# A decoder on one core: seven block products for the cross attention's queries and for three quarters of the shared expert

## The chip, the cores and the metric

The kernel runs on one core of one Trainium2 chip. The metric is the time of one execution on the device in microseconds (us); a version is judged by the median of several runs. All arithmetic is float32.

## The reference, cut to what matters

Two decoder layers work on x of 8 batches x 256 tokens x 256 features. Layer 0 is self attention, a cross attention and an expert layer; layer 1 starts with a causal self attention. None of these is touched. What follows in layer 1 is (a function per batch b, P = 128):

```python
xn = layernorm(x[b])                      # 256 x 256
k, v = split(ctx[b] @ Wkv)                # ctx 256 x 512, Wkv 512 x 2048
q = xn @ Wq                               # Wq 256 x 1024, 16 heads of 64
o = softmax([q . null_key, q . k^T] / 8) @ [null_value; v]
x[b] += layernorm(o @ Wout, 1e-6) * ln_scale + ln_bias
# then, over all 2048 tokens
xe = layernorm(x)
gates, expert = top1(sigmoid(xe @ router))
routed = swiglu(xe * gates; w1, w3, w2 of that token's expert)
shared = (silu(xe @ ws1) * (xe @ ws3)) @ ws2          # ws1, ws3 256 x 704
out = x + routed + shared
```

## The kernel before

**Stages.** Layer 0 and layer 1's self attention run as units up to about 624 us. Then `null_cross_attention` (from line 1057) goes over the eight batches, then `token_experts` (from line 1423) finishes: rows are sorted by expert through HBM, 17 tiles go through their experts (`slots`), and x gets what comes back.

**A batch in the loop (from L1359).** `weighted` makes the scores (`stx`, L1228), their exponentials (ScalarE, L1232), the sums `den` (L1242) and the weighted values `ox` (L1266). Then the norm of the next batch is transposed (`layernorm_T`, tile `xn`), and the normed rows of the batch before for the experts (`routed_norm` and `routed_rows`, tile `xne`); both tiles share one tag with two buffers. Then come the next batch's keys and values. These two products are not done plainly: `seven` cuts left and right matrix into 2 x 2 blocks and makes seven block products in place of eight, with sums of blocks on both sides (`sums_of_context`, `sums_of_weights` on VectorE, DVE for short) and additions of the results when they leave PSUM. `k7` and `v7` are generators that issue these products in steps; a product that goes on in a bank must wait until ScalarE or DVE has read what stood there. The queries are plain: `queries` (L1205) makes the null key's scores `nps` and 64 half matmuls `fm`, whose results DVE copies to `qTx` (L1069). `divide` multiplies the attention by the reciprocals that come back through HBM (`rs`). `outward` (L1321) projects it (`wo`), ScalarE copies the result (`yx`, L1329), DVE takes its statistics, GpSimd (POOL) raises the variance to -1/2 (`lxrs`, L256), DVE norms, POOL multiplies by `lns` and adds `lnb` (L1334, L1335) and adds to x (L1336).

**Order.** Between `manual_schedule` and `order.close()` the order of TensorE (PE) is that of the code. Elsewhere, and for the other engines inside the loop, a planner picks among what it takes to be ready, earlier lines first, and the result is fixed in each engine's queue. On the chip a queue never overtakes: an instruction that waits holds up those behind it. Buffers of one tag are given out in the order of the code.

**Shared expert.** Its 2048 tokens are done in four quarters of 512 (`hidden_shared`, L947): 5 full chunks of 128 hidden features take 4 matmuls of 128x512 each, the last 64 features of both weights 2; ScalarE applies silu (L944), DVE multiplies (L945) into `mid`. Quarter 0 covers the last batch's division, quarter 1 its norm and the routing; there the tiles are called `hx`. Quarters 2 and 3 (`h`) stand in `token_experts`, quarter 3 as the last thing before the final output matmuls (L1442, L1453) and stores. In the last stage an expert's weights lie in tiles `w13` and `w2`, four buffers each.

In the profile a float32 matmul counts as two instructions, and `product` (L272) issues each matmul as two halves of 64 output rows that run side by side, so one product of a 128x128 block is four.

Of the kernel before, what the change touches and what calls it, by code (L numbers as in the profile page):

```python
# [38 lines left out]
P = 128  # L39
# [116 lines left out]
def plain(  # L156
# [105 lines left out]
    def layernorm_T(b, work, mm):  # L262

        xn = work.tile([P, 2, D], F32, tag="xn", name="xn")
        mv, rs = norm_stats([x[:, 2 * b + t, :] for t in range(2)], 1e-5, small, "ln")
        for t in range(2):
            last = normed(xn[:, t, :], x[:, 2 * b + t, :], mv, rs, t)
        return last, transposed(xn, work, mm, "xnT")
# [9 lines left out]
    def transposed(rows, work, mm, tag, dst=None):  # L278

        ps = mm.tile([P, 2, 2 * P], F32, tag="mm", name="tr")  # L280
        for t in range(2):
            for c in range(2):
                nc.tensor.transpose(ps[:, c, t * P : (t + 1) * P], rows[:, t, c * P : (c + 1) * P], ident)  # L283
        if dst is None:
            dst = work.tile([P, 2, 2 * P], F32, tag=tag, name=tag)
        nc.scalar.copy(dst, ps)  # L286
        return dst
# [472 lines left out]
    def weights_x():  # L760
# [4 lines left out]
        ctxs = wproj.enter_context(tc.tile_pool(name="ctxs", bufs=2, side="right"))  # L765
# [191 lines left out]

    def routed_norm(b, work):

        xn = work.tile([P, 2, D], F32, tag="xn", name="xne")  # L960
        mv, rs = norm_stats([x[:, 2 * b + t, :] for t in range(2)], 1e-5, small, "ln")
        for kept, v in zip(norms[b], (mv, rs)):
            nc.gpsimd.tensor_copy(kept, v)
        for t in range(2):
            normed(xn[:, t, :], x[:, 2 * b + t, :], mv, rs, t)
        return xn
# [90 lines left out]
    def null_cross_attention(phase):  # L1057
# [4 lines left out]
        def feature(dst, w, rows, copy, c2):  # L1062

            n = w.shape[1]
            ps = mm.tile([P, 2, S], F32, tag="mm", name="fm")
            for i in range(2):
                for cc in range(n):
                    product(ps[:, i, :], w[:, cc, (c2 + i) * P : (c2 + i + 1) * P], rows[:, cc, :], cc == 0, cc == n - 1)
            copy(dst[:, c2 : c2 + 2, :], ps)  # L1069

        def features(dst, w, rows, copy):
            for c2 in range(0, nc8, 2):
                feature(dst, w, rows, copy, c2)
# [6 lines left out]
        def keys(ctxT):  # L1080
            kT = work.tile([P, nc8, S], F32, tag="kT", name="kTx", bufs=1)
            features(kT, wkv_x, ctxT, nc.scalar.copy)
            return kT

        half = CTX // P // 2

        def w_block(j, k):

            return wkv_x.rearrange("p c (m k f) -> p c m k f", m=2, k=2)[:, half * j : half * (j + 1), :, k, :]

        tw = wsum.tile([P, 3, half, 2, XH * XD // 2], F32, name="tw")
        t1, t2, t3, t4 = tw[:, 0], tw[:, 1], w_block(0, 1), tw[:, 2]

        def sums_of_weights(n):
            dst, p, q = (
                (t1, w_block(0, 1), w_block(0, 0)),
                (t2, w_block(1, 1), t1),
                (t4, w_block(1, 0), t2),
                (t3, w_block(1, 1), w_block(0, 1)),
            )[n]  # L1100
            for m in range(2):
                for c in range(half):
                    nc.vector.tensor_tensor(dst[:, c, m], p[:, c, m], q[:, c, m], ALU.subtract)

        def sums_of_context(ctxT):


            def block(i, j):
                return ctxT[:, half * j : half * (j + 1), bass.ts(i, P)]

            sw = wsum.tile([P, 3, half, P], F32, tag="sw", name="sw")
            s1, s2, s3, s4 = sw[:, 0], sw[:, 1], block(1, 0), sw[:, 2]
            nc.vector.tensor_tensor(s1, block(1, 0), block(1, 1), ALU.add)
            nc.vector.tensor_tensor(s2, s1, block(0, 0), ALU.subtract)
            nc.vector.tensor_tensor(s4, block(0, 1), s2, ALU.subtract)
            nc.vector.tensor_tensor(s3, block(0, 0), block(1, 0), ALU.subtract)
            return block(0, 0), block(0, 1), s4, block(1, 1), s1, s2, s3

        w_terms = w_block(0, 0), w_block(1, 0), w_block(1, 1), t4, t1, t2, t3

        def seven(terms, m, dst):

            xy = scp.tile([P, 2, 2 * S], F32, tag="sc", name=f"kv{m}")
# [8 lines left out]
            def product_of(n, bank, fresh):  # L1132

                s, t = terms[n - 1], w_terms[n - 1][:, :, m, :]
                for i in range(4 if m == 0 else 1):
                    for c in range(half):
                        if m == 0:
                            args = bank[:, bass.ts(i, P)], t[:, c, bass.ts(i, P)], s[:, c, :]
                        else:
                            args = bank, s[:, c, :], t[:, c, :]  # L1140
                        for made in product(*args, fresh and i == 0 and c == 0, c == half - 1):
                            for other in (xb, yb):
                                for ins in read[id(other)] if other is not bank else ():
                                    tc.declare_no_dep(made.ins, ins.ins, reason="another bank")

            if m == 0:
# [7 lines left out]
            else:  # L1154

                def of(i, j):
                    return dst[:, i, 8 * j : 8 * j + 8, :]

                def seen(bank):
                    return bank.rearrange("p (h d) -> p h d", h=8)  # L1160

            def kept(bank, name):
                t = work.tile([P, 2 * S], F32, tag="pT", name=f"kv{name}{m}", bufs=4)
# [6 lines left out]
            zb = mm.tile([P, 2 * S], F32, tag="mm", name=f"kvz{m}")  # L1170
# [12 lines left out]
            reads(yb, nc.vector.tensor_tensor(of(0, 1), u, seen(yb), ALU.add))  # L1183
            product_of(4, xb, False)
# [3 lines left out]
        def vals(ctxT):  # L1188
            v = work.tile([P, 2, XH, XD], F32, tag="vx", name="vx", bufs=1)
# [13 lines left out]
            return v  # L1203

        def queries(xnT):  # L1205

# [5 lines left out]
            yield  # L1212
            qT = work.tile([P, nc8, S], F32, tag="qT", name="qTx", bufs=1)
            for c2 in range(0, nc8, 2):
                feature(qT, wq_x, xnT, nc.vector.tensor_copy, c2)
                if c2 == 0:
                    yield
            yield qT, en
# [102 lines left out]
        def outward(b, oT, en):  # L1321
# [9 lines left out]
            for t in range(2):  # L1331
                xt = x[:, 2 * b + t, :]
                normed(y[:, t, :], y[:, t, :], mv, rs, t)
                nc.gpsimd.tensor_tensor(y[:, t, :], y[:, t, :], lns, ALU.mult)  # L1334
                nc.gpsimd.tensor_tensor(y[:, t, :], y[:, t, :], lnb, ALU.add)  # L1335
# [6 lines left out]
        def silu(n):  # L1342
            return work.tile([P, 2 * S], F32, tag="pT", name="slx", bufs=4)[:, :n]

        def quarter(q):
            return hidden_shared(q, pair, silu)


        _, xnT = layernorm_T(0, work, mm)
        ctxT = context(0)  # L1350
        kT = keys(ctxT)
        for n in range(3):
            sums_of_weights(n)
        v = vals(ctxT)
        *_, (qT, en) = queries(xnT)
        sums_of_weights(3)
        load_router()
        order = ExitStack()
        for b in range(B):  # L1359
# [4 lines left out]
            if more:  # L1364
                _, xnT = layernorm_T(b + 1, work, mm)
                terms = sums_of_context(ctxT)
            else:
                rest()
# [4 lines left out]
                routing_tables(late)  # L1373
                order.enter_context(tc.manual_schedule(engines={mybir.EngineType.PE}))
            if b:
                routed_rows(b - 1, routed_norm(b - 1, work), work)
            if more:
                order.enter_context(tc.manual_schedule(engines={mybir.EngineType.PE}))
                kT = work.tile([P, nc8, S], F32, tag="kT", name="kTx", bufs=1)
                v = work.tile([P, 2, XH, XD], F32, tag="vx", name="vx", bufs=1)  # L1380
                k7, v7, q = seven(terms, 0, kT), seven(terms, 1, v), queries(xnT)
# [7 lines left out]
            if more:  # L1389

                for made in (k7, k7, v7, k7, k7, v7, v7):
                    next(made)
                if b:
                    routed_scores(b - 1)
                next(q)
                next(v7)
                next(v7)
            else:
                for i, _ in enumerate(quarter(0)):
# [4 lines left out]
            if more:  # L1404
                *_, (qT, en) = q
            order.close()
        with tc.manual_schedule(engines={mybir.EngineType.PE, mybir.EngineType.DVE}):
            for i, _ in enumerate(quarter(1)):
                if i == 1:
                    xn = routed_norm(B - 1, work)  # L1410
                if i == 2:
                    routed_rows(B - 1, xn, work)
                if i == 3:
# [9 lines left out]
    def token_experts(phase):  # L1423
# [21 lines left out]

        def quarter(q):
            for last in hidden_shared(q, pair, silu):
# [1189 lines left out]
```

## Time and profile before

| what | value |
| --- | --- |
| runs | 1377.36, 1377.01, 1377.0, 1373.41, 1374.71 us; median 1377.0 |
| profiled execution | 1376.14 us; its span, first to last instruction, 1374.4 us |
| granted clock, mean | 0.995 |
| busy, of the span | PE 97%, weight loads 66%, DVE 39%, ScalarE 33%, POOL 29% |
| one batch of the loop | 60.4 us (from 780.34 to 840.73 us and on), of which PE idles 0.32 us |
| queries of one batch, `fm` | 64 instructions of 128x256, 57.0 us in all for eight batches |
| quarters of the shared expert | `hx` 88 instructions of 128x512, 38.9 us; `h` 88, 38.2 us |

A row of the timeline has the start, the busy time, the engine, the line, the operation, the tile written <- tiles read, the shapes, the count, and in brackets the idle time of the engine before it and what ended that. A row of PE ends about 0.2 us after the next may begin, so the cost of a group is taken from its start to the start of the next.

### The profile page before, as it was taken

To read this page: it belongs to the slowest core of one execution; us is meant where nothing else is said; L and a number is where in the kernel's file an instruction comes from. 1 tells how busy PE (TensorE), PEld (TensorE's weight loads), DVE (VectorE), ACT (ScalarE), POOL (GpSimd) and SP (SyncE) were. 2 spreads that over 40 slices of the span, in tenths; PEclk is the share of its full clock that TensorE was granted. 3 is DMA by queue.
4 is the path that set the end of the run, shared out by engine and by line. 5 is a ranking of instruction groups with operands and counts; after the bars stand their busy time and mean duration, and the time that the engine had idled before them with its cause. 6 is when DMAs were issued, how large, how long until landed. Compare 5 with 4: busy or idle time off the path is not lost.

```text
span 1374.4 us, 30022 instructions
## 1 busy us (share of the span) xinstructions
PE 1334.7 (97%) x12814; PEld 901.9 (66%) x12814; DVE 533.9 (39%) x1539; ACT 456.8 (33%) x730; POOL 405.0 (29%) x513
## 2 busy tenths in 40 slices
PE   6999999999999999999999999999999999999998
PEld 3666756756766766764757566676756655788884
DVE  5443563473465555344223322232332236322223
ACT  2455443543553443431313222131322212022221
POOL 4322052051033243320324424152343512400004
PEclk9999999999999999999999999999999999999999
DMA  9970000000000004200011010101101110689954
GB/s 304 339 232 16 9 25 1 17 24 1 2 9 2 2 9 141 83 2 1 21 44 33 16 32 16 48 2 47 33 1 32 64 32 26 273 331 403 392 199 129
DMA packets 46926, 116.65 MB, mean 85 GB/s; under 512 B 8272, under 2 KB 30400, under 8 KB 42432
## 3 DMA queue, kind: packets, MB, share of 16 engines
q1 hardware_dynamic: 38912, 92.74, 19.9%
q0 software_dynamic: 5152, 18.89, 3.7%
q10 hardware_dynamic: 2720, 3.02, 0.6%
q8 instruction: 103, 1.69, 0.5%
q14 instruction: 39, 0.32, 0.1%
HBM read 104.00 MB, written 27.93 MB: 96 GB/s over the span
## 4 chain that ended last, share of the span: by engine, by line
PE 85%; DVE 5%; POOL 4%; issue 2%; ACT 1%; DMA 0%; ACTq 0%; POOLq 0%; DVEq 0%; SPq 0%
PE kv L274 11%; PE st L334 9%; PE o L366 9%; PE h L274 6%; PE fm L274 5%; PE wo L274 5%; PE ox L1266 4%; PE stx L1228 4%; PE out L1625 3%; PE out L1442 3%; PE h L952 3%; PE tr L283 3%; PE qk L274 3%; PE hx L952 3%; PE den L1242 2%; PE ao L274 2%
## 5 line engine op out<-in xcount | busy, mean ns | idle before, releaser
L366 PE MATMUL o<-pT,padv 128*64 128x256 f32 (+1 forms) x1536 | 172.1, 366 | 1.2 <-POOL pT L346 1.2
L343 ACT ACTIVATE pT<-st 128x1024 f32<-128x1024 f32 (+1 forms) x128 | 110.4, 915 | 88.2 <-PE st L334 87.4
L366 PEld LDWEIGHTS o<-pT,padv 128*64 128x64 f32 x1536 | 103.3, 137 | 53.9 <-issue 11.2
L334 PE MATMUL st<-qm,kT 64*128 64x256 f32 (+1 forms) x1024 | 116.3, 365 | 0.9 <-DVE qm L312 0.6
L334 PEld LDWEIGHTS st<-qm,kT 64*128 64x128 f32 x1024 | 89.2, 188 | 25.9 <-issue 15.6
L1234 POOL TENSOR_TENSOR both<-pTx 128x512 f32<-128x512 f32 x64 | 79.7, 1280 | 55.5 <-ACT pTx L1232 38.9
L1232 ACT ACTIVATE pTx<-stx 128x1024 f32<-128x1024 f32 x64 | 62.0, 1021 | 88.2 <-PE stx L1228 87.6
L274 PE MATMUL h<-xrT,w 128*64 128x128 f32 (+1 forms) x1936 | 87.0, 250 | 1.2 <-issue 1.2
L274 PEld LDWEIGHTS h<-xrT,w 128*64 128x64 f32 x1936 | 84.4, 137 | 4.0 <-issue 1.8
L256 POOL TENSOR_TENSOR lnrs<-lnve,mhalf 128x2 f32<-128x2 f32 x48 | 33.6, 701 | 150.9 <-DVE lnve L254 99.1
L343 ACT ACTIVATE pT<-st,kbias 128x1024 f32<-128x1024 f32 x64 | 68.0, 1112 | 28.8 <-PE st L334 28.7
L334 PE MATMUL st<-qm,memk 64*128 64x256 f32 x512 | 68.8, 393 | 0.5
L945 DVE TENSOR_TENSOR midr<-sl,h 128x128 f32<-128x128 f32 x102 | 29.3, 288 | 101.8 <-PE h L274 69.0
L944 ACT ACTIVATE sl<-h 128x128 f32<-128x128 f32 (+1 forms) x114 | 35.3, 310 | 96.0 <-PE h L274 56.5
L1228 PE MATMUL stx<-qTx,kTx 64*128 64x256 f32 x512 | 64.3, 391 | 2.5 <-ACT pTx L1232 2.5
L346 POOL TENSOR_SCALAR_AFFINE_SELECT pT<-pT 128x512 f32<-128x512 f32 x64 | 39.5, 638 | 83.0 <-ACT pT L343 79.8
L274 PE MATMUL qk<-l_wqkv,xnT 128*64 128x512 f32 x256 | 62.8, 612 | 0.7 <-ACT xnT L286 0.7
L1266 PE MATMUL ox<-pTx,vx 128*64 128x256 f32 x512 | 61.1, 381 | 0.0
L1228 PEld LDWEIGHTS stx<-qTx,kTx 64*128 64x128 f32 x512 | 46.1, 186 | 20.3 <-issue 9.2
L274 PE MATMUL wo<-wout_x,oT 128*64 128x256 f32 x512 | 58.0, 379 | 0.0
L334 PEld LDWEIGHTS st<-qm,memk 64*128 64x128 f32 x512 | 48.0, 186 | 15.1 <-issue 5.1
L1317 POOL TENSOR_TENSOR oT<-oT,rs 128x512 f32<-128x512 f32 x30 | 37.7, 1286 | 65.7 <-DMA rs<-rd 65.7
(312 smaller groups left out, 2222.1 us busy)
## 6 DMA issues: line engine op xcount, KB each, us to landing
w<-packs SPq DMA_DIRECT2D x22, 1408.0 KB
w<-packs SPq DMA_DIRECT2D x22, 768.0 KB
rs<-rd SPq DMA_DIRECT2D x16, 512.0 KB
packs<-L_ffn_w_eDF SPq DMA_DIRECT2D x8, 704.0 KB
packs<-L_ffn_w_eDF SPq DMA_DIRECT2D x8, 640.0 KB
packs<-L_ffn_w_eFD SPq DMA_DIRECT2D x8, 640.0 KB
ctxT<-ctx_T SPq DMA_DIRECT2D x8, 512.0 KB
wkv_x<-L_xattn_Wkv POOLq DMA_DIRECT2D x1, 4096.0 KB, 18.8
```

The costliest lines, as they stand in the source:

```text
L274: nc.tensor.matmul(out[h], lhsT[:, h], rhs, start=start, stop=stop, skip_group_check=True)
L283: nc.tensor.transpose(ps[:, c, t * P : (t + 1) * P], rows[:, t, c * P : (c + 1) * P], ident)
L334: nc.tensor.matmul(st[:, g, i, :n], kT[rows, c, bass.ts(kt, P)], qm[rows, 2 * mq + i, c, q0:], start=True, stop=True,)
L343: nc.scalar.activation(pT[:, :, :, :n], st[:, :, :, :n], AF.Exp, scale=scale, **kb)
L366: nc.tensor.matmul(o[64 * i : 64 * i + 64, mq, q0:], v_pad[:, kt, 4 * c + 2 * mq + i, 2 * g : 2 * g + 2, :], pTs[kt][:, g, i, : S - q0], s ...
L952: nc.tensor.matmul(h, shared["ws13"][:, c, lo : lo + P], shared["xnT"][:, c, bass.ts(q, 2 * S)], start=c == 0, stop=c == 1)
L1228: nc.tensor.matmul(st[:, g, kt, :], kT[rows, c, bass.ts(kt, P)], qT[rows, c, :], start=True, stop=True)
L1232: nc.scalar.activation(pT, st, AF.Exp, scale=scale)
L1234: nc.gpsimd.tensor_tensor(both, pT[:, :, 0, :], pT[:, :, 1, :], ALU.add)
L1266: nc.tensor.matmul(o[XD * g : XD * (g + 1), i, :], v[:, kt, 2 * (c2 + i) + g, :], pT[:, g, kt, :], start=kt == 0, stop=kt == 1, skip_group ...
L1442: nc.tensor.matmul(ps, mid[:, i, lo : lo + P], w2[:, i, :], start=i == 0, stop=i == NFC - 1)
L1625: nc.tensor.matmul(ps[h], mid[:, i, h], sets[k % len(sets)][1][:, i, :], start=i == 0, stop=i == NFC - 1, skip_group_check=True,)
```

## The change

1. **Queries.** `seven` gets a name, the terms of both sides and a flag for the layout, and makes the queries as well (`q7`): seven products of 4 x 1 blocks with 128 columns each in place of the 64 instructions of `fm`. Sums of Wq are made once (tile `twq`), sums of the normed rows for each batch on DVE (`swq`, four of 128x128). ScalarE now takes four of the results out of PSUM and DVE three, where DVE copied four. The first batch's queries stay plain.
2. **Order in the loop.** `q7`'s steps are woven between those of `k7` and `v7`; products 7, 3 and 4 come after `outward`, with the routing scores ahead of 4 and the null key's scores behind it. `routed_norm` is issued directly after `layernorm_T`, and `routed_rows` comes into PE's written order.
3. **Buffers.** `ctxT`, `xnT` and the tag `xn` (norm of the next batch and rows for the experts) have one buffer in place of two.
4. **Output norm.** The multiplication by `lns` and the addition of `lnb` go from POOL to DVE.
5. **Shared expert, quarters 0, 1 and 3.** `hidden_seven` makes the 5 full chunks of both weights in seven products, two chunks at a time (a, b, then c with one), 35 matmuls of 128x256 in place of 20 of 128x512; the last 64 features stay as they were. DVE makes four sums of the weights (128x640) before quarters 0 and 3 (quarter 1 uses the first ones) and four of the rows (128x256) for each quarter.
6. **End of the loop.** In the last batch `divide` and `outward` come after 15 of the 21 products of quarter 0; in quarter 1 the norm, the transposes and the scores of the last batch come one step earlier.

The core of the diff:

```diff
-    def layernorm_T(b, work, mm):
-        xn = work.tile([P, 2, D], F32, tag="xn", name="xn")
+    def layernorm_T(b, work, mm, bufs=2):
+        xn = work.tile([P, 2, D], F32, tag="xn", name="xn", bufs=bufs)
...
-        ctxs = wproj.enter_context(tc.tile_pool(name="ctxs", bufs=2, side="right"))
+        ctxs = wproj.enter_context(tc.tile_pool(name="ctxs", bufs=1, side="right"))
...
+    def hidden_seven(q, of_w, sx, mm, pair, spare):
...
+        def chunks(first, n):
+            xb, yb = pair(n * S)
+            (p1, p5), (u, sl) = ([t[:, k, : n * S] for k in range(2)] for t in (spare(), spare()))
...
+            product_of(1, xb, True)
+            read[id(xb)].append(nc.scalar.copy(p1, xb))
+            yield
+            zb = mm.tile([P, 2 * S], F32, tag="mm", name="hz")[:, : n * S]
+            product_of(2, zb, True)
+            nc.vector.tensor_tensor(p1, p1, zb, ALU.add)
+            nc.scalar.activation(p1, p1, AF.Silu)
+            yield
+            product_of(5, yb, True)
+            read[id(yb)].append(nc.scalar.copy(p5, yb))
+            yield
+            product_of(6, xb, False)
+            read[id(xb)].append(nc.scalar.copy(u, xb))
+            yield
+            product_of(7, xb, False)
+            read[id(xb)].append(nc.vector.tensor_tensor(p5, p5, xb, ALU.add))
+            yield
+            product_of(3, yb, False)
+            read[id(yb)].append(nc.vector.tensor_tensor(u, u, yb, ALU.add))
+            to_mid(0, u, p1)
+            yield
+            product_of(4, xb, False)
+            nc.scalar.activation(sl, xb, AF.Silu)
+            yield to_mid(1, sl, p5)
...
+        a, b = chunks(0, 2), chunks(2, 2)
+        for g in (a, a, a, a):
+            next(g)
+        yield
+        for g in (b, a, b, a):
+            next(g)
+        yield
+        for g in (b, a, b):
+            next(g)
+        c = chunks(4, 1)
+        yield
+        for g in (c, b, c, b):
+            next(g)
+        yield
+        for g in (c, b, c):
+            next(g)
+        ht = mm.tile([P, 2 * S], F32, tag="mm", name="ht")
+        end(0)
+        yield
+        next(c), next(c)
+        end(1)
+        last = next(c)
...
     def routed_norm(b, work):
-        xn = work.tile([P, 2, D], F32, tag="xn", name="xne")
+        xn = work.tile([P, 2, D], F32, tag="xn", name="xne", bufs=1)
...
-                nc.gpsimd.tensor_tensor(y[:, t, :], y[:, t, :], lns, ALU.mult)
-                nc.gpsimd.tensor_tensor(y[:, t, :], y[:, t, :], lnb, ALU.add)
+                nc.vector.tensor_tensor(y[:, t, :], y[:, t, :], lns, ALU.mult)
+                nc.vector.tensor_tensor(y[:, t, :], y[:, t, :], lnb, ALU.add)
...
             if more:
-                _, xnT = layernorm_T(b + 1, work, mm)
-                terms = sums_of_context(ctxT)
+                _, xnT = layernorm_T(b + 1, work, mm, 1)
+                if b:
+                    xe = routed_norm(b - 1, work)
+                of_ctx = sums_of_rows(ctxT, CTX // P // 2, "sw", False)
...
             if b:
-                routed_rows(b - 1, routed_norm(b - 1, work), work)
+                routed_rows(b - 1, xe, work)
             if more:
-                order.enter_context(tc.manual_schedule(engines={mybir.EngineType.PE}))
...
+                of_x = sums_of_rows(xnT, 1, "swq", True)
...
+                q7 = seven("q7", of_x, w_terms(q_blocks, 0), qT, False)
                 next(k7)
                 rest()
...
-                for made in (k7, k7, v7, k7, k7, v7, v7):
+                for made in (k7, k7, v7, k7, k7, k7, v7, v7, q7, v7, q7, v7, v7, q7):
                     next(made)
-                if b:
-                    routed_scores(b - 1)
-                next(q)
-                next(v7)
-                next(v7)
             else:
-                for i, _ in enumerate(quarter(0)):
+                shared["of_w"] = sums_of_shared(*(sums.tile([P, full * P], F32, name=f"tws{i}") for i in range(4)))
+                first = quarter(0)
+                for i in range(4):
+                    next(first)
                     if i == 0:
                         routed_scores(b - 1)
             divide(oT, rs, (nc.gpsimd, nc.gpsimd if more else nc.vector))
             outward(b, oT, old)
             if more:
-                *_, (qT, en) = q
+                next(q7), next(q7)
+                if b:
+                    routed_scores(b - 1)
+                next(q7)
+                en = null_key(xnT)
+            else:
+                for _ in first:
+                    pass
             order.close()
...
+        def beside():
+            return wts.tile([P, 2, FIRST], F32, tag="w13", name="beside")[:, :, : 2 * S]
...
+            sets = [wts.tile([P, NFC * D], F32, tag="w2", name=f"sums{i}") for i in range(3)]
```

A step of `seven` issues, call by call, the products 1 | 2 and 5 | 6 | 7 | 3 | 4; its evictions are ScalarE copies after 1, 5, 6 and 4 and DVE additions after 2, 7 and 3.

## The prediction

> **What bounds the kernel.** I read the page's busy shares first, then PE's timeline over one batch of the loop, then DVE's queue at the place where the change puts new evictions.
>
> ```profile
> PE 1334.7 (97%) x12814; PEld 901.9 (66%) x12814; DVE 533.9 (39%) x1539; ACT 456.8 (33%) x730; POOL 405.0 (29%) x513
> ...
> L274 PE MATMUL fm<-xnT,wq_x 128*64 128x256 f32 x512 | 57.0, 379 | 0.0
> L952 PE MATMUL hx<-xnTe,ws 128*128 128x512 f32 x88 | 38.9, 596 | 0.0
> ...
> 833.73 7.08 PE L274 MATMUL fm<-xnT,wq_x 128*64 128x256 f32 x64
> 840.73 2.00 PE L1228 MATMUL stx<-qTx,kTx 64*128 64x256 f32 x16
> ...
> 858.83 0.66 PE L283 MATMUL tr<-ident,xn 128*128 128x128 f32 x4
> 859.33 0.60 PE L283 MATMUL tr<-ident,xne 128*128 128x128 f32 x4
> 859.86 1.97 PE L274 MATMUL kv<-ctxT,wkv_x 128*64 128x128 f32 x32
> ...
> 869.47 1.92 PE L274 MATMUL kv<-ctxT,wkv_x 128*64 128x128 f32 x32
> 871.22 1.92 PE L274 MATMUL kv<-sw,wkv_x 128*64 128x128 f32 x32
> ```
>
> PE is full and no row here has idle time in brackets, so a matmul taken out is time taken out, and a wait put in is time put in. The clock was 0.995, so it plays no part. DVE and ScalarE have room in sum; what counts is the moment at which an eviction gets its turn.
>
> **Gains.** Queries: `fm` costs 840.73 - 833.73 = 7.00 us a batch, 64 instructions of 256 columns at 109 ns. The keys' products already have the shape of `q7`: from 869.47 to 871.22, 32 instructions of 128 columns, 54.7 ns each, half of 109, so a short matmul pays no extra. `q7` has 7 x 16 = 112 of them: 6.13 us, 0.87 less, for seven batches **6.1 us**.
>
> The Trainium skill ("TensorE: Matmul & The Clock Gate", Back-to-back issue gap) speaks against that: in a stream of weight loads and matmuls it gives some 81 ns a matmul at 128 columns and 131 at 512, so halving the columns doesn't halve the cost; by it 112 x 81 = 9.1 us would stand against the 7.0 of `fm`, a loss of some 15 us in seven batches. The trace has 54.7 ns for this very shape, side by side in halves, and decides.
>
> Shared expert: quarter 0 takes 434.7 ns for an instruction of 128x512 (36 of them from 1105.84 to 1121.49), so its 44 cost 19.13 us. The same full array at 256 columns stands in the output matmuls: the 84 from 1181.33 to 1199.46 take 216 ns each. A quarter then has 70 x 216 + 4 x 434.7 = 16.9 us, 2.2 less, for three quarters **6.5 us**. Further, the transposes of the last batch's rows waited 0.49 us at 1140.47. Now `outward` comes earlier with 4.8 us of products behind it and 3.5 of quarter 1, and the chain to the rows loses POOL's slower steps, so that wait goes: **0.5 us**. Together 13.1.
>
> **First cost, the shared buffer of xn and xne.** Rows for the experts can be normed only when the transposes of `xn` have read the one buffer, and PE's order has the transposes of `xne` next. The DVE copy of `ox` before it ends at 859.64, one norm instruction takes 0.41, the handover 0.08 (as at 8.03 to 8.12): PE goes on at 860.13 where it went on at 859.33, and the second half waits a little more, 0.84 us. Behind it in PE's queue stands everything of the next products. It falls on batches 1 to 6: **5.0 us**. Nothing: only if the transposes of `xn` were drawn ahead of the last `ox`, and PSUM tiles of their tag are given out in order. I keep 0 and 6 as ends.
>
> **Second cost, the eviction after q7's seventh product.** Product 4 goes on in the bank of product 7 and must wait for DVE's addition. Between stand product 3 (0.87 us) and, from batch 1 on, the scores (0.43); the addition takes 0.69 and 0.3 for both handovers. Were DVE free, nothing would wait. But `outward` has just ended, and DVE has its norm:
>
> ```profile
> 834.56 0.75 DVE L251 BATCH_NORM_STATS2 lxst<-yx 128x6 f32<-128x256 f32 x2 [7.95 <-ACT yx L1329]
> 835.23 0.30 DVE L252 BATCH_NORM_AGGREGATE lxmv<-lxst 128x2 f32<-128x6 f32 x2
> 835.56 0.17 DVE L254 TENSOR_SCALAR lxve<-lxmv 128x2 f32<-128x2 f32 x1
> 836.55 0.74 DVE L260 TENSOR_SCALAR yx<-yx,lxmv,lxrs 128x256 f32<-128x256 f32 x2 [0.81 <-POOL lxrs L256]
> 837.20 0.69 DVE L1069 COPY qTx<-fm 128x512 f32<-128x512 f32 x1
> 840.09 0.75 DVE L251 BATCH_NORM_STATS2 lnst<-x 128x6 f32<-128x256 f32 x2 [2.21 <-POOL x L1336]
> 840.76 0.67 DVE L1069 COPY qTx<-fm 128x512 f32<-128x512 f32 x1
> 841.35 0.17 DVE L252 BATCH_NORM_AGGREGATE lnmv<-lnst 128x2 f32<-128x6 f32 x1
> ```
>
> With t the end of `wo` (833.73), the statistics end at t + 1.5, the variance at 2.0, the norm starts at 2.8. Three places are open. Between statistics and aggregate, as the copy at 840.76 stands: addition until 2.24, product 4 at 2.3 instead of 2.18, 0.12 us a batch, and 0.7 in batch 0, which has no scores. In POOL's gap before the norm: until 2.7, waits of 0.62 and 1.05. Behind all six instructions that the norm now has on DVE (two at 0.37, four additions or multiplications at about 0.34): from 4.9 to 5.6, waits of 3.5 and 3.9. I take the first place, since product 7 is ready after 0.9 us where the first copy of `fm` was ready after 1.75: 6 x 0.12 + 0.7 = **1.4 us**; ends 0 and 25.
>
> **Third cost, waits in the quarters.** (a) ScalarE changes its table between exp and silu, 1.28 us (at 1105.42); so far the chunk of 3.5 us covered it. Now it stands before silu of chunk a's sum, and the copies of products 5 and 6 behind it: product 6 ends 3.5 us after the quarter's start, product 7 may start after scores and b1 at 4.8, its copy is done at about 5.8: 1.0 us, once. (b) In each quarter a7 waits for the copy of a6 behind silu and another copy (0.1), and b7, with only c1's 0.43 us ahead, for a copy of 0.59 plus 0.28 of handovers: together 0.5, three times. (c) After quarter 1 the PSUM banks pass to the next stage; there PE waited 0.84 us; now a silu of 256 columns (0.37) stands before the last one: 0.4 more. Sum **2.9 us**; ends 0.5 and 6.5, the whole gain of the quarters.
>
> **At nothing.** The sums on DVE, 39% busy: four of 128x512 for Wq (0.69 each), eight of 128x640 (0.85, scaled from 0.69), twelve of 128x256 (0.42), four of 128x128 a batch (0.29); Wq's lie beside the 36 us of first products, in which DVE has 14.6 (624 to 660 us). Should the weights' sums before quarter 3 (3.4 us, waiting for `w2` buffers until about 1328) hold up the experts' multiplications, each costs up to 0.3. ScalarE's 2.3 us a batch more: it has 15.7 of 60.4. The copy of product 4 (0.59 and 0.3) lies under the null key's 0.9; the next score after that under a wait of 0.32 that exists anyway. One buffer of `ctxT`: its 512 KB are issued on SP about 8.6 us before t and needed some 28 later; the slowest comparable load, 1 MB, landed after 10.3. Behind it on SP stand only the next reciprocals. One `xnT`: its last reader is done 18 us before. The earlier last `outward` needs `rs` (landed at 1113.24) and the first POOL product (1.28); PE gets there at about 1115.5. POOL's 16 gathers after the last expert keep their time, the last is issued at 1361.40 and lands 2.8 later; its addition stood at 1366.06 and would now come at about 1364.4; were it late, up to 0.5.
>
> **Sum.** The query part comes out even (-6.1 + 5.0 + 1.4), so the gain is that of the quarters. 1376.1 (profiled, 0.9 below the median) - 13.1 + 5.0 + 1.4 + 2.9 = 1372.3; on the median of 1377.0, a difference of -3.8 gives **1373.2 us**.
>
> **Rivals.**
>
> 1. *The norm in the way.* The addition after product 7 stands behind the output norm on DVE. For it: DVE never overtakes, and copies of `fm` that were ready did stand behind instructions waiting for POOL (2.21 us at 840.09). Against: the product is ready before the norm's variance is. Place: between q7's products 3 and 4, seven times. Without this cost the sum is -5.2, so it decides from 0.75 us a batch. POOL's gap gives 4.8 us, 1376.6, even; behind the two norm instructions 2.15 a batch, 1387; behind all six, 1396. Chance 0.24 (slower 0.20, same 0.04).
> 2. *The shared buffer costs nothing,* or DVE norms earlier than I think, or the quarters run without waits: 1373.2 - 5 = 1368, with both 1365.3. For it: one early transposition is enough. Against: the order of PSUM tiles. Chance 0.19, faster.
> 3. *The seven products of the quarters don't do what they should:* each product waits for the eviction of its bank, and the 6.5 us are lost: 1373.2 + 3.6 = 1377, with the sums of weights in the way 1380. For it: for two chunks ScalarE and DVE have five evictions each, of 0.6 to 0.7 us, where they had two. Against: two chunks are interleaved, and 3.0 and 3.5 us stand beside 6.1 of products. Chance 0.12 (same 0.05, slower 0.07).
>
> **Chances.** The forecast, 1371 to 1377 with its own spread, has 0.45 (faster 0.27, same 0.18). Faster by over 0.2%, that is below 1374.2: 0.27 + 0.19 = 0.46. Within 0.2%, about what a measurement of this kernel can tell from no change: 0.18 + 0.04 + 0.05 = 0.27. Slower: 0.20 + 0.07 = 0.27. The range: 1365.3 of rival 2 is nearly the floor, so 1366; above, 1386 takes in rival 3 and most of rival 1 up to the norm's two instructions, and leaves out the place behind all six.
>
> **What would show it.** PE's 128-column rows of `q7` at 54.7 ns, 112 a batch, and no `fm` after the first; a wait of about 0.8 us on PE before the transposes of `xne`, by DVE L260, six times; a wait before q7's last product, by DVE's addition, of 0.1 or of over 0.6; quarters of 17 us plus half a microsecond. By the sum a batch of the loop stays at 60.4 to 60.5 us; over 61 the query part gives back more than it brings, and under 60 one of the two waits isn't there: in both the forecast is wrong. So would waits by DMA before the sums of the context, for which I have put nothing.

## The result and the profile after

The change makes no difference to speak of: 1376.6 us as the median of 26 runs (1374.1 to 1381.0) against 1375.9 of 48 runs of the kernel before (1373.4 to 1377.9); the ratio is 1.0006, interval 1.0001 to 1.0011, so if anything it is slower. The forecast was 1373.2, a gain of 0.28%. The profiled execution took 1377.69 us, its span is 1375.9, the clock 0.994.

The page of the changed kernel begins so; the columns are busy time, share of the span and instructions of each engine.

```profile
PE 1328.1 (97%) x13240; PEld 932.5 (68%) x13240; DVE 580.9 (42%) x1646; ACT 487.6 (35%) x788; POOL 384.8 (28%) x481
```

PE is busy for 6.6 us less than the 1334.7 of before, and the span is 1.5 longer: PE stands still for 8.1 us more. Where, is read from marks that both timelines have. The loop and the two stretches behind it repeat to 0.02 us between profiles of one program, so each difference there can be placed (us; the forecast's terms beside it):

| from - to | before | changed | difference | forecast |
| --- | --- | --- | --- | --- |
| first `stx` of batch 0 - of batch 7 (the loop) | 421.86 | 423.66 | +1.80 | +0.3 |
| - first transpose of `xne` (last batch's attention) | 18.96 | 21.17 | +2.21 | 0 |
| - `counts` (quarters 0 and 1, last `outward`) | 49.17 | 45.62 | -3.55 | -2.9 |
| - first expert's `h` | 52.17 | 52.48 | +0.31 | +0.4 |
| - quarter 3 (the experts) | 136.18 | 137.40 | +1.22 | 0 |
| - its output products (quarter 3) | 18.99 | 17.58 | -1.41 | -1.7 |
| - end of the span | 16.64 | 17.52 | +0.88 | 0 |

The start of the loop moved by 0.04 between these two profiles; between two profiles of one program it moves by 0.6 to 0.8. The sum is +1.5, the difference of the spans.

**The loop.** PE's timeline over the turn of a batch, changed kernel:

```profile
837.05 1.92 PE L274 MATMUL q<-swq,wq_x 128*64 128x128 f32 x32
838.80 0.59 PE L274 MATMUL sc<-router,xnTe 128*64 128x8 f32 x16
839.35 1.09 PE L274 MATMUL q<-xnT,twq 128*64 128x128 f32 x16
840.27 1.03 PE L274 MATMUL nps<-xnT,wn 128*64 128x256 f32 x8
841.24 2.00 PE L1330 MATMUL stx<-qTx,kTx 64*128 64x256 f32 x16
...
859.34 0.66 PE L283 MATMUL tr<-ident,xn 128*128 128x128 f32 x4
860.66 0.67 PE L283 MATMUL tr<-ident,xne 128*128 128x128 f32 x4 [0.67 <-ACT xnT L286]
861.26 1.97 PE L274 MATMUL k<-ctxT,wkv_x 128*64 128x128 f32 x32
```

From the transposes of `xn` to the first keys pass 1.92 us; before it was 859.86 - 858.83 = 1.03. That is the wait for the shared buffer, 0.89 a batch. The bracket names ScalarE's copy of `xn`, but PE's next instructions read `xne`; DVE's queue at that moment shows when that is made:

```profile
859.46 0.69 DVE L1376 COPY oT<-ox 128x512 f32<-128x512 f32 x1 [6.57 <-PE ox L1368]
860.11 0.73 DVE L260 TENSOR_SCALAR xne<-x,lnmv,lnrs 128x256 f32<-128x256 f32 x2
```

The norm starts at 860.11, behind the copy of `ox`, and PE goes on 0.55 later, when the first half is there. From the start of the transposes of `xn` that is 1.32 us; the forecast, in the times of the kernel before, had 860.13 - 858.83 = 1.30.

**The last batch.** Three views of the changed kernel, DVE, POOL, PE, and behind them PE and POOL in the kernel before:

```profile
1089.87 0.41 DVE L979 TENSOR_TENSOR sx<-xnTe,sx 128x256 f32<-128x256 f32 x1
1090.89 2.77 DVE L260 TENSOR_SCALAR xne<-x,lnmv,lnrs 128x256 f32<-128x256 f32 x2 [0.61 <-POOL lnrs L256]
...
1096.84 1.49 DVE L979 TENSOR_TENSOR sx<-xnTe,sx 128x256 f32<-128x256 f32 x1
1098.25 3.72 DVE L964 TENSOR_TENSOR tws<-ws 128x640 f32<-128x640 f32 x2
1101.89 2.76 DVE L964 TENSOR_TENSOR tws<-ws,tws 128x640 f32<-128x640 f32 x2
1104.56 1.28 DVE L1376 COPY oT<-ox 128x512 f32<-128x512 f32 x2
```

```profile
1092.24 1.26 POOL L1336 TENSOR_TENSOR both<-pTx 128x512 f32<-128x512 f32 x1
...
1093.77 9.33 POOL L1336 TENSOR_TENSOR both<-pTx 128x512 f32<-128x512 f32 x6
```

```profile
1092.23 0.65 PE L1344 MATMUL den<-both,hot 128*64 128x256 f32 x4
1093.56 0.65 PE L1344 MATMUL den<-both,hot 128*64 128x256 f32 x4 [0.67 <-POOL both L1336]
1094.04 1.90 PE L1368 MATMUL ox<-pTx,vx 128*64 128x256 f32 x16
...
1103.03 1.03 PE L1344 MATMUL den<-both,hot 128*64 128x256 f32 x8
1105.30 0.65 PE L283 MATMUL tr<-ident,xne 128*128 128x128 f32 x4 [1.24 <-DVE oT L1376]
```

```profile
1090.39 1.08 PE L1242 MATMUL den<-both,hot 128*64 128x256 f32 x8
1091.30 1.90 PE L1266 MATMUL ox<-pTx,vx 128*64 128x256 f32 x16
...
1100.29 1.03 PE L1242 MATMUL den<-both,hot 128*64 128x256 f32 x8
1101.25 0.66 PE L283 MATMUL tr<-ident,xne 128*128 128x128 f32 x4
```

```profile
1090.65 5.01 POOL L1234 TENSOR_TENSOR both<-pTx 128x512 f32<-128x512 f32 x4
```

The planner has put the sums for the shared expert (`sx`, `tws`) among the last batch's attention, where POOL adds (`both`). While POOL adds, a DVE instruction that reads two SBUF operands, and the norm too, takes its own time and a little less than one of POOL's additions more: `sx` 1.49 instead of 0.41, `tws` 1.86 instead of 0.82 (the time alone is seen below, in e2), the norm 1.39 instead of 0.37; POOL's addition takes 1.56 instead of 1.25. Behind them in DVE's queue stand both copies of `ox`, whose PSUM tiles PE needs for the transposes: a wait of 1.24 us. Another of 0.67 is for POOL at `den`. Start to start the first `den` takes 1.81 instead of 0.91, the last with the wait behind it 2.27 instead of 0.96: 0.90 and 1.31, together the whole 2.21.

### The profile page after: what moved, and what is told of

Its sections match the earlier page's. It is cut to its first block, busy times and chain, and to the rows that moved or that the text cites. A ratio compares the mean times of both kernels' runs of the same rounds, so it can differ in the third digit from the quotient of the medians.

```text
span 1375.9 us, 31067 instructions
## 1 busy us (share of the span) xinstructions
PE 1328.1 (97%) x13240; PEld 932.5 (68%) x13240; DVE 580.9 (42%) x1646; ACT 487.6 (35%) x788; POOL 384.8 (28%) x481
## 4 chain that ended last, share of the span: by engine, by line
PE 81%; DVE 6%; POOL 5%; issue 3%; ACT 1%; DMA 1%; SPq 0%; POOLq 0%; ACTq 0%; DVEq 0%
PE st L334 9%; PE o L366 9%; PE h L274 6%; PE v L274 6%; PE k L274 5%; PE wo L274 4%; PE ox L1368 4%; PE stx L1330 4%; PE out L1750 3%; PE out L1559 3%; PE tr L283 3%; PE qk L274 3%; PE q L274 2%; PE den L1344 2%; PE ao L274 2%
## 5 line engine op out<-in xcount | busy, mean ns | idle before, releaser
L944 ACT ACTIVATE sl<-h 128x128 f32<-128x128 f32 (+1 forms) x108 | 31.8, 295 | 80.6 <-PE h L274 56.3
```

## Experiments

Ratios are to the kernel before, run beside each kernel on the same chip, with 95% intervals.

**e1_own_buffer.** The rows for the experts get the buffer of the output rows, which is free then.

```diff
-        xn = work.tile([P, 2, D], F32, tag="xn", name="xne", bufs=1)
+        xn = work.tile([P, 2, D], F32, tag="y", name="xne", bufs=1)
```

> The changed kernel, but the normed rows for the experts (xne) share the buffer of the output rows (yx), which nobody needs at that time, and no longer that of xn. Theory (the shared buffer costs what was forecast): the changed kernel has 1.92 us from the transposes of xn to the first product of the keys and the kernel before had 1.03; the 0.89 go in batches 1 to 6, 5.3 us, so 1376.6 - 5.3 = 1371.3, and a batch of the loop takes 59.8 us instead of 60.7. Rival (the wait is for ScalarE's copy of xnT, as the row of the waits names it, or something else is late at once): the time stays within 1 us of 1376.6.

1370.2 us, ratio 0.996 (0.9948 to 0.9972). A batch takes 59.82 us instead of 60.72, the last batch's attention 21.17 as in the changed kernel. PE at the place of the wait:

```profile
856.47 0.66 PE L283 MATMUL tr<-ident,xn 128*128 128x128 f32 x4
856.96 0.60 PE L283 MATMUL tr<-ident,xne 128*128 128x128 f32 x4
857.49 1.97 PE L274 MATMUL k<-ctxT,wkv_x 128*64 128x128 f32 x32
```

1.02 us instead of 1.92. The shared buffer costs what was forecast, and ScalarE's copy was not the cause.

**e2_sums_later.** Two of the `tws` wait for POOL's last addition, the other two and quarter 1's `sx` are queued behind the reciprocal (`inv`).

```diff
+            made = nc.vector.tensor_tensor(dst, p, q, ALU.subtract)
+            if inv is not None:
+                kind, other = (Sync, shared["both"]) if (dst is t1 or dst is t2) else (NoSync, inv)
+                tc.add_manual_dep(made.ins, other.ins.name, DependencyInfo(kind, DATA), reason="later")
...
-        with tc.manual_schedule(engines={PE, DVE}):
+        with tc.issue_after(inv.ins), tc.manual_schedule(engines={PE, DVE}):
```

> The changed kernel, with another order of VectorE's queue in the last batch alone: the first two of the four sums of the shared expert's weights wait for the last addition on POOL (both), the other two and the sums of rows for quarter 1 stand behind the reciprocal. Theory (the sums slow POOL and are slowed by it, and the last copies of ox stand behind them): the stretch from the last batch's first scores to the transposes of xne goes from 21.2 back to about 19.0 us, the 1.24 us of waiting there are gone, and the time is 1376.6 - 2.2 = 1374.4. Rival (the sums themselves are late for quarter 0, or the waits of 0.67 at den come from POOL's own queue): the stretch shortens by at most 1 us and quarter 0 gets new waits before its products 5, 7 or 4; time 1376 to 1377.

1375.3 us, ratio 0.9999 (0.999 to 1.0008); the stretch is 19.85. DVE (lines lie 5 further down), then POOL:

```profile
1098.53 0.69 DVE L1381 COPY oT<-ox 128x512 f32<-128x512 f32 x1 [2.33 <-PE ox L1373]
1103.75 0.82 DVE L964 TENSOR_TENSOR tws<-ws 128x640 f32<-128x640 f32 x1 [4.53 <-POOL both L1341]
1104.61 0.82 DVE L964 TENSOR_TENSOR tws<-ws,tws 128x640 f32<-128x640 f32 x1
1105.79 0.69 DVE L1381 COPY oT<-ox 128x512 f32<-128x512 f32 x1 [0.35 <-PE ox L1373]
```

```profile
1096.31 7.41 POOL L1341 TENSOR_TENSOR both<-pTx 128x512 f32<-128x512 f32 x6
```

The wait of 1.24 is gone, the sums take 0.82 and the additions 1.24 each; the copy from PSUM at 1098.53 runs beside POOL in its usual 0.69. Theory and rival were each right in part: 1.3 of 2.2 came back and the wait of 0.67 at `den` stayed. In the total 1.3 us are less than the interval's width of 2.5, so the ratio alone would not show them.

**e4_quarters_alone** and **e5_queries_alone** are the two halves of the change: the kernel before with `hidden_seven` for quarters 0, 1 and 3 and the moved `outward`; and the changed kernel with plain quarters in the old order. The first edit is of the kernel before, the second of the changed one:

```diff
-            return hidden_shared(q, pair, silu)
+            sx = sums.tile([P, 4, S], F32, tag="sx", name="sx", bufs=2)
+            return hidden_seven(q, shared["of_w"], sx, mm, pair, spare)
```

```diff
-            sx = sums.tile([P, 4, S], F32, tag="sx", name="sx", bufs=2)
-            return hidden_seven(q, shared["of_w"], sx, mm, pair, spare)
+            return hidden_shared(q, pair, silu)
```

> The kernel before, with the quarters' part of the change alone: quarters 0, 1 and 3 by seven products, the last output projection inside quarter 0; queries, buffers and norms as before. Theory (by the trace: quarters 0 and 1 with their passage to the next stage gain 3.2, quarter 3 gains 1.4, the last batch's attention loses 2.2 to the sums, the experts' stage loses 1.2): 1375.9 - 1.2 = 1374.7. Rival 1 (the forecast's own sum): 1375.9 - 6.5 - 0.5 + 2.9 = 1371.8. Rival 2 (the loss in the last batch and in the experts' stage comes from the queries' part): 1375.9 - 4.6 = 1371.3, with no wait at the transposes of the last batch's rows.

> The changed kernel with plain quarters: the shared expert as before, all in pairs of 512 columns, the last output projection behind quarter 0 as before; queries by seven products, one buffer, norms on VectorE as changed. Theory (by the trace, 1.8 us more by the start of the last batch's attention): 1375.9 + 1.8 = 1377.7. Rival 1 (the forecast's sum, even): 1375.9 + 0.3 = 1376.2. Rival 2 (the queries' part also causes the losses behind the loop): 1375.9 + 1.8 + 2.2 + 1.2 = 1381.

The quarters alone take 1371.2 us, ratio 0.9971 (0.9962 to 0.9981), the queries alone 1376.7, ratio 1.001 (0.9999 to 1.002). The quarters bring 4 us, which is near the forecast's sum for them (1371.8) and near rival 2 (1371.3); my theory, read from the trace of the whole change, gave them too little. That the forecast's sum comes out is partly luck: the last batch's attention loses 0.99, which it had not, and the experts' stage, which it left alone, is 1.06 shorter in this profile. The queries cost 1.4, between theory and forecast; the interval just takes in no difference at all.

The halves do not add up: -4.2 and +1.4 against the +0.7 of the whole. By the profiles 4.0 us are added where both meet, 0.9 in the last batch's attention, 2.4 in the experts' stage and 0.8 at the end (on the last two see e9 to e11). By stages, the last batch's attention loses 0.99 with the quarters alone, 0.34 with the queries alone, and 2.21 with both: only with both is DVE so late that the sums keep PE waiting for the copies of `ox` ahead of the transposes.

**e6_buffer_and_sums** is both repairs, the two diffs above; **e7_rows_later** also moves quarter 0's `sx` behind POOL's additions and the reciprocal:

```diff
+        for n, made in enumerate(rows if inv is not None else ()):
+            later(made, inv, n < 2)
```

> Both repairs in one kernel: the rows for the experts in the output rows' buffer, and the last batch's sums behind POOL's additions and the reciprocal. Theory (the two losses are separate): the loop keeps 59.82 us a batch and the stretch from the last scores to the transposes of xne 19.85, so that by stages it is 5.4 + 1.3 = 6.7 below the changed kernel: 1369.9, a ratio to the kernel before of 0.9955. Rival (the gain of the first repair is swallowed where the experts' weights arrive, whatever comes ahead): the experts' stage grows by what is saved, ratio 0.998 or more.

> Both repairs, and also quarter 0's four sums of rows go behind POOL's additions (two of them) and the reciprocal (two), so that the statistics and the norm of xne and with them POOL's first additions come earlier. Theory (the 0.67 us of waiting at den is POOL standing behind lnrs, which waits for VectorE's statistics between sums of rows): the stretch goes from 19.85 to about 19.1 us, ratio to the kernel before 0.995. Rival (POOL is late because of the output norm on VectorE and its own memsets, not because of the sums): the 0.67 stays, and a new wait for the sums of rows comes before product 5 or 3 of quarter 0.

They take 1368.6 us, ratio 0.9948 (0.9936 to 0.9961), and 1369.3, ratio 0.9957 (0.9945 to 0.9969). The repairs add up: a batch takes 59.82 and the last attention 19.86. With the later rows the last attention takes 19.31, quarters 0 and 1 unchanged at 45.62; these 0.55 us are too few to show between the two totals. PE at the first `den` in e7:

```profile
1085.74 1.43 PE L1356 MATMUL den<-both,hot 128*64 128x256 f32 x8
1087.00 1.90 PE L1380 MATMUL ox<-pTx,vx 128*64 128x256 f32 x16
```

It takes 1.26 where the kernel before takes 0.91, so 0.35 of the 0.90 stay, as in e5 (0.34), which has none of these sums: POOL's first addition begins 6.17 us after the first scores instead of 5.68. This much of the rival is right, and belongs to the queries' part. Both kernels beat the kernel before by some 6 to 7 us.

**e8_norms_on_pool** is e7 with `lns` and `lnb` on POOL again.

```diff
-                nc.vector.tensor_tensor(y[:, t, :], y[:, t, :], lns, ALU.mult)
-                nc.vector.tensor_tensor(y[:, t, :], y[:, t, :], lnb, ALU.add)
+                nc.gpsimd.tensor_tensor(y[:, t, :], y[:, t, :], lns, ALU.mult)
+                nc.gpsimd.tensor_tensor(y[:, t, :], y[:, t, :], lnb, ALU.add)
```

> Both repairs and the later sums of rows, but the output norm's scale and bias (lns, lnb) stand on POOL again, as in the kernel before the change. Theory (the move to VectorE buys nothing on the path, since the rows are needed 18 us later): the loop stays at 59.8 us a batch, and the time within 1 us of the kernel with both repairs and later sums. Rival (forecast: the shorter chain to the rows takes away a wait): 0.5 us come back at the transposes of the last batch's rows in quarter 1, and xne is late in the loop, 0.3 or more a batch.

1378.3 us, ratio 1.0022 (1.0013 to 1.0031): 9 us more, against theory and rival. A batch takes 61.12 us, the last attention 22.81. PE's waits between 655 and 1350 us, in e8 and then in e7 (total, times, longest):

```profile
PE den L1356 <- POOL both L1348: 7.3, 13, 1.2
PE stx L1342 <- ACT pTx L1346: 2.5, 8, 0.3
```

```profile
PE stx L1342 <- ACT pTx L1346: 2.5, 8, 0.3
PE h L274 <- issue: 2.1, 1, 2.1
```

In e8 POOL begins its additions 11.5 us after the end of the output projection (848.18 - 836.70); in the kernel before it was hardly earlier (845.04 - 833.73 = 11.3), but there 7.0 us of `fm` stood between projection and scores. With q7 woven among keys and values it is 4.2, and POOL is late. On DVE the chain takes 9.1 (843.25 - 834.19 in e7). So without the move of the norm's scale and bias the queries' gain would be lost; in these kernels it is worth 1.3 us a batch and 3.5 in the last attention.

**e9_plain_quarter3** is the changed kernel with `hidden_shared` in quarter 3; **e10_changed_again** and **e11_before_again** are second profiles of the two kernels.

```diff
-            for last in hidden_seven(q, of_w, sx, mm, pair, beside):
+            for last in hidden_shared(q, pair, silu):
```

> The changed kernel, but quarter 3 in the last stage as it was, in pairs of 512 columns, without sums; everything else as changed. Theory (the longer experts' stage, 137.4 us against 136.2, and the longer end, 17.5 against 16.6, are the scatter of transfers and not quarter 3): the stage from the first expert's products to quarter 3 takes 135 to 137.5, quarter 3 takes 19.0 instead of 17.6, so 1376.6 + 1.4 = 1378.0. Rival (the sums for quarter 3, in the experts' buffers, hold up the experts' weights or the last gathers): the stage is 1.2 shorter and the end 0.9, so 1376.

> The changed kernel once more, unchanged, for a second profile of it. Theory (what the stages before the loop, the experts' stage and the end add is scatter between executions): the loop and the stretches up to the experts agree with the first profile to 0.05 us, the experts' stage (137.4 then) falls anywhere between 135 and 137.5, and the end from quarter 3's output products on (17.5 then) anywhere between 16.6 and 17.8. Rival (they belong to the program): the stage takes 137.2 to 137.6 again, the end 17.4 to 17.6.

> The kernel before once more, for a second profile of it. Theory (scatter): the experts' stage (136.2 then) falls anywhere between 135 and 137.5, the end from quarter 3's output products on (16.6 then) anywhere between 16.6 and 17.8. Rival (they belong to the program): 136.0 to 136.4 and 16.6 to 16.7 again.

e9: 1376.9 us, ratio 1.0008 (0.9999 to 1.0017), experts' stage 136.75, end 17.16. The total lies between theory and rival, and stage and end are 0.65 and 0.36 shorter than in the changed kernel, half or less of what the rival says, so it does not decide. e10: 1376.8 us, stage 137.31, end 17.59. e11: 1375.1, 135.70 and 16.70. The end falls where the rival put it both times, the stage only in e10. PE's waits from 1150 to 1345 us in e10, then in e11:

```profile
PE h L274 <- issue: 1.9, 1, 1.9
PE out L1750 <- issue: 1.4, 1, 1.4
```

```profile
PE h L274 <- issue: 1.1, 1, 1.1
...
PE out L1625 <- issue: 0.8, 1, 0.8
```

The end repeats to 0.1 us for either program and so belongs to the program, not to chance. After the last store's issue it lasts 5.6 to 5.8 us in before, e4, e5 and e11, 6.2 in e9 and 6.5 to 6.8 in all others; behind that issue the traces have 5 loads of code in the first four and 6 or 7 in the others, some of them only after the span. Whether they lengthen the end or only go with it stays open, and with it what makes these 0.9 us.

The experts' stage took 135.1 to 136.2 us without the queries' part (before, e4, e11), 136.1 to 137.4 with it. There PE waits, in most kernels twice, for nothing that the rows name, while the DMA engines are 0.84 busy. The packets of the traces say more. In all twelve profiles each of these waits, 23 in sum, ends 1.2 to 1.6 us after a load of 16 KB on the queue `q8 instruction` has ended: in the changed kernel the loads end at 1222.30 and 1295.02, and PE goes on at 1223.81 and 1296.46. And the waits stand at places in PE's own queue. Counted along the trace, with weight loads and the sequencer's own, PE goes on with its instructions 21697 and 24258 in both profiles of the kernel before, and 768 further on, give or take one, in both of the changed kernel, in e1, e2 and e6 to e9. In e5 they are 1536 further, and in e4 one wait alone falls into the stage, 1792 beyond the first: all multiples of 256. This is how waits for code that comes late would look; no run moved these loads, so it is not shown by an experiment. The waits make 0.65 of the 1.22 us between the first two profiles and 1.3 of the 1.6 between e11 and e10, and without them the stage takes 133.6 to 134.4 us in all twelve. Why the loads come later in one execution than in another stays open.

## Why the forecast was wrong

**The step that failed** is the paragraph "At nothing", in its sentence on the sums on DVE. It took DVE's load over the span (39%) and the instructions' times from places where POOL was idle, and never asked where in DVE's queue the sums would stand. They stood in the last batch's attention, took 1.9 us instead of 0.8 (`tws`) and 1.5 instead of 0.4 (`sx`) beside POOL, slowed POOL too, and held up the copies of `ox`. Placed elsewhere they gave back 1.3 us (e2) and 0.55 (e7), together 1.9 us where the forecast had 0. The other 0.35 of this stretch is POOL's later start, which the forecast had not either.

This is not all. The loop costs 1.5 us more than forecast, and 2.1 us were lost in the experts' stage and at the end, where nothing was forecast: 0.65 of them are the waits beside the loads of code, the rest is open. Together that is 5.8; the quarters came out 0.45 better (0.65 and 0.1 better up to the experts, 0.3 worse in quarter 3), so by stages 5.4 us are missing, between -3.9 and +1.5. By the medians (+0.7) 4.5 are missing. And the forecast counted from 1377.0, the median of five runs; 48 runs of the kernel before have 1375.9.

**Gains.** Right in the main. q7's products take 0.91, 0.87, 0.87, 0.88, 1.75 and, once the wait is over, 0.92 us: 6.2 against 6.13 forecast and 7.00 of `fm`. Two groups beside them take longer in the new order: `nps` 0.97 instead of 0.90, a `v` product behind `q` 1.77 instead of 1.72; that the change of shape does it was not tested. The instruction of 128 columns costs 54.7 ns here too. The Trainium skill ("TensorE: Matmul & The Clock Gate", Back-to-back issue gap) has 81 ns for 128 columns; the measurement decides. Without its waits a quarter takes 17.2 us, forecast 16.9. The wait for the last batch's rows is gone, as forecast.

**First cost, the buffer.** Right: 0.89 instead of 0.84, and e1 took it away.

**Second cost, q7's fourth product.** Right in place and size. DVE's addition stands at 838.64, behind the statistics and the first aggregate and ahead of the norm; scores to product 4 take 0.55 instead of 0.43, so 0.12. In batch 0 it is 0.55 (0.38 in the bracket) instead of 0.7. The rest of the loop's excess, 0.24 a batch, is 0.05 of the buffer, 0.07 of q7's products and 0.12 of the two groups beside them.

**Third cost, waits in the quarters.** The table load cost 0.1 at most instead of 1.0. It did not wait for the sum that silu reads: it ran from 1107.80, right behind the copy of product 1, while DVE made that sum from 1107.88 to 1108.51, so only 0.6 of its 1.28 us came on top. The other waits cost, start to start, 0.46 and 0.50 in quarter 0 (0.21 and 0.35 in the brackets), 0.41 in quarter 3 (0.15) and next to nothing in quarter 1: 1.4 in sum, forecast 1.5. Two of them are b7 behind ScalarE's copy, as forecast; the 0.50 is the last product of quarter 0 behind DVE's addition, which the forecast had not. The passage to the next stage costs 0.31 for 0.4.

**The rivals.** The norm was not in the way of product 7; e8 shows that the same chain decides elsewhere, at POOL's additions, which no rival named. "The shared buffer costs nothing" is refuted by e1, "the quarters don't do what they should" by e4, where they bring 4 us.

**A page against the row.** The Trainium skill ("SBUF — State Buffer", Who interferes with whom) says that VectorE instructions with two SBUF inputs, and copies and scalar operations in a faster mode, contend with a GpSimd instruction that reads SBUF, and that one blocks until the other is through. The rows agree: 0.41 + 1.08, 0.82 + 1.04, 0.37 + 1.02 us beside additions that take 1.25 alone, and a copy from PSUM keeps its 0.69 (e2). The forecast weighed the sums without this, though the additions stood in the trace of before.

## What to carry to other kernels

Work "beside" an engine with room must be given a place in that engine's queue: ask what it runs next to and which short copy stands behind it. A shorter product also moves what follows it nearer to the chain ahead, so a chain that was hidden with ease (here output norm, x, rows, POOL's additions) has to be timed again. And before two tiles share a buffer to save space, look for a tile that is dead at that time: here one word gave back 5 us and more.

## What the runs showed of the hardware

VectorE and GpSimd slowed each other: 128x256 sums went from 0.41 to 1.49 us, 128x640 sums from 0.82 to 1.86, POOL's additions from 1.25 to 1.56, while copies from PSUM kept their 0.69. The bracket behind a wait can name the wrong engine: "0.67 <-ACT xnT" was a wait for DVE's norm, as e1 shows by taking it away. TensorE's unnamed waits in the experts' stage, 0.7 to 2.1 us, each end 1.2 to 1.6 us after a 16 KB load of code and keep their places in its queue. And a program's last 5.6 to 6.8 us, after the last store is issued, repeat to 0.1 us for the two programs that were profiled twice, and differ by about 1 us between programs.
